# The last stage of a two-part image kernel: three column groups in a turn, a smaller output tile, and TensorE in program order

## The chip, the core and the metric

The kernel runs on one core of a Trainium2 chip, as one program. The metric is the device time of one execution in microseconds; the time shown is the median of several runs. A profile is a record of one execution: for each instruction on each engine its start and its length. The engines named here are TensorE (PE; its weight loads are PEld), VectorE (DVE), ScalarE (ACT), GpSimd (POOL) and SyncE (SP). They run side by side, each works through its own instructions in order, and they wait for each other by semaphores. TensorE writes its results into PSUM, which has eight banks of 128 x 512 floats; another engine has to read a bank out before it can be written again.

## What is computed

The input x has the shape (4, 64, 256, 256). Two layers follow each other. The first is an attention and feed-forward block with convolutions, and fills the first three quarters of the time. The second works on 64 channels (E) of every pixel and does linear attention along the rows, then the same along the columns, then a two-layer network. The last stage of the kernel does the column attention and the network. Cut to that, for the values of one column, with x of 256 rows and 64 channels:

```python
q = elu(n @ wq.T + bq) + 1          # 4 heads, one value each; n = layernorm(x)
k = elu(n @ wk.T + bk) + 1
v = n @ wv.T + bv                   # 4 heads of 16
q = q / q.mean(rows); k = k / k.sum(rows)
o = q * (k * v).sum(rows)
x = x + o @ wo.T + bo
x = x + gelu(layernorm(x) @ w1.T + b1) @ w2.T + b2
```

The output is x as (4, 64, 256, 256), with channels ahead of rows and columns.

## The kernel before

The kernel runs in five stages, and only the last, `stage_d`, is changed. It reads the result of the row attention from the scratch tensor `hd` in DRAM and writes `out`.

**Tiling.** There are 4 images and 8 groups of 32 columns in each, so 32 groups, in the list `seq`. A group is one tile `h` of 128 partitions by 32 columns by 2 row halves by 64 channels: the partition is the row in a half. A loop over `r` from 0 to 7 goes through a group four columns at a time.

**Two generators.** `attn` (L1178) does the attention of a group, and `ffn` (L1276) the network of the group before. `_steps` takes them forward in turn, from one `yield` to the next. A pass of the outer loop (L1316) is called a turn: it loads the next group, runs `attn` for group n and `ffn` for group n - 1, and after every second group it stores.

`attn` has these parts:
- For each r it transposes four blocks of `h` (L1188), copies the result out on ScalarE to `xT` (L1190) and multiplies by the query and key weights (L1197, "scores"). After four r the scores are turned on VectorE (L1201). Beside this runs `spread`, which takes the sum over channels (L1163), subtracts the mean (L1165), squares on ScalarE (L1167) and sums again (L1168), to give the variance. `rstd` takes the root on ScalarE (L1173) and the reciprocal (L1175).
- The scores are scaled and shifted (L1204, L1205), `feature` applies min and Exp, L1214 makes `f`, and L1217 makes `kz`, the weighted keys.
- L1223 sums keys times `h` over the rows. L1227 and L1230 give the sums of f and the turned queries. VectorE makes `z` and `zn` (L1234 to L1241), TensorE turns it (L1244), `mix` applies the value and output weights (L687), and VectorE makes `bdm` (L1250).
- L1256 and L1259 make the attention's output, in four PSUM banks for each row half, and L1262 adds it into `h`.
- `spread` and `rstd` again, and L1273 gives `xf`, the normalised tile that the network reads.

`ffn` turns four blocks of `xf` (L1283), copies to `xfT` (L1285), does the first layer in four PSUM banks (L1296) with Gelu on ScalarE (L1298), puts the residual `h` (L1304) and the second layer (L1307) into one bank, and VectorE adds the bias b2 and writes the bank to the output tile `st` (L1309). The write is turned: four columns next to each other in `st`, for 128 rows, so that consecutive writes lie 256 bytes apart. `st` holds two groups, that is 64 columns, and GpSimd's queue sends it out in eight DMAs of 512 KB (L1332) with runs of 256 bytes in DRAM.

**What sets the order.** The program's text gives the instructions and what they depend on. The order in which each engine gets them is set by the framework's scheduler when the kernel is built, by priorities and estimated durations. Tiles of one name share a fixed number of buffers (`bufs`), and an instruction that writes a tile waits until its buffer is free. PSUM is shared out by two helpers: `mm()` gives one of six banks and `sm()` one of two.

Of the kernel before, what the change touches and what calls it, by code (L numbers as in the profile page):

```python
# [9 lines left out]
F32 = mybir.dt.float32  # L10
AF = mybir.ActivationFunctionType
ALU = mybir.AluOpType
# [235 lines left out]
def kernel(ctx: ExitStack, tc: tile.TileContext, x, packs, fd, out, off):  # L248
# [8 lines left out]
    def mm():  # L257
        return ps.tile([128, 512], F32, tag="mm", name="mm")

    def sm():  # L260
        return ps.tile([128, 512], F32, tag="sm", name="sm", bufs=2)
# [33 lines left out]
    def bc(ap, n):  # L295

        return ap.unsqueeze(2).to_broadcast([ap.shape[0], ap.shape[1], n])
# [826 lines left out]
    def stage_d():  # L1124
        with ExitStack() as cs:
# [25 lines left out]
            V.memset(one, 1.0)  # L1151

            def load(b, g):
                h = p.tile([128, 32, 2, C], F32, name="h", bufs=3)
                for rh in (0, 1):
                    for j in (0, 1):
                        SY.dma_start(h[:, 16 * j:16 * j + 16, rh, :], hd[b, rh * 128:(rh + 1) * 128, :, 2 * g + j, :])
                return h

            def spread(src, n, s2):  # L1160

                s1 = p.tile([128, n], F32, tag="ln_s", name="ln_s")
                V.tensor_reduce(s1, src, AX.X, ALU.add)  # L1163
                xc = p.tile([128, n, C], F32, tag="xc", name="xc")
                V.scalar_tensor_tensor(xc, bc(s1, C), -LN_S, src, ALU.mult, ALU.add)  # L1165
                sq = p.tile([128, n, C], F32, tag="ln_sq", name="ln_sq")
                S.activation(sq, xc, AF.Square)  # L1167
                V.tensor_reduce(s2, sq, AX.X, ALU.add)  # L1168
                return xc

            def rstd(s2, n):
                s3 = p.tile([128, n], F32, tag="ln_d", name="ln_d")
                S.activation(s3, s2, AF.Sqrt, bias=eps_t, scale=LN_S)  # L1173
                s4 = p.tile([128, n], F32, tag="ln_r", name="ln_r")
                V.reciprocal(s4, s3)  # L1175
                return s4

            def attn(h, xfs):  # L1178

                qp = p1.tile([128, 32, 32], F32, name="qp")  # L1180
                v1 = p1.tile([128, 64], F32, name="v1")
                for r in range(8):
                    if r % 2 == 0:
                        k = r // 2
                        spread(h[:, 8 * k:8 * k + 8].rearrange("p c a e -> p (c a) e"), 16, v1[:, 16 * k:16 * k + 16])
                    t = mm()
                    for i in range(4):
                        T.transpose(t[:, i * 128:(i + 1) * 128], h[:, r * 4 + i].rearrange("p a e -> p (a e)"), ident)  # L1188
                    xT = p.tile([128, 512], F32, name="xT")
                    S.copy(xT, t)  # L1190
                    yield
                    if r % 4 == 0:
                        qk = sm()


                    for g in range(4):
                        T.matmul(qk[g * 32:(g + 1) * 32, r % 4 * 128:r % 4 * 128 + 128], cwt, xT.rearrange("p (c n) -> p c n", c=4)[:, :, g * 32:(g + 1) * 32],  # L1197
                                 start=True, stop=True)
                    if r % 4 == 3:

                        V.transpose(qp[:, r // 4 * 16:r // 4 * 16 + 16].rearrange("p c m -> p (c m)"), qk)  # L1201
                rs = rstd(v1, 64)
                u = qp[:, :, 0:16].rearrange("p c (r k) -> p c r k", r=2)
                V.tensor_tensor(u, u, bc4(rs, 2, 8), ALU.mult)  # L1204
                V.tensor_tensor(u, u, cbq.unsqueeze(1).unsqueeze(1).to_broadcast([128, 32, 2, 8]), ALU.add)  # L1205
                yield
                e = feature(p1, u, [128, 32, 2, 8])
                yield
                f = p1.tile([128, 2, 2, 32, 4], F32, name="f")
# [2 lines left out]
                for rh in (0, 1):  # L1212
                    for k in (0, 1):
                        V.scalar_tensor_tensor(f[:, rh, k], uv[:, rh, :, k * 4:k * 4 + 4], 1.0, ev[:, rh, :, k * 4:k * 4 + 4], ALU.add, ALU.max)  # L1214
                fv = f.rearrange("p r k c h -> p r k (c h)")
                kz = p1.tile([128, 2, 128], F32, name="kz")
                V.tensor_tensor(kz.rearrange("p r (c h) -> p r c h", h=4), f[:, :, 1], rs.rearrange("p (c r) -> p r c", r=2).unsqueeze(3).to_broadcast([128, 2, 32, 4]), ALU.mult)  # L1217
                yield

                t = mm()  # L1220
                for rh in (0, 1):
                    for g in range(4):
                        T.matmul(t[g * 32:(g + 1) * 32, :], kz[:, rh, g * 32:(g + 1) * 32], h[:, 8 * g:8 * g + 8, rh, :], start=(rh == 0), stop=(rh == 1))  # L1223
                qs = sm()
                for k in (0, 1):
                    for rh in (0, 1):
# [36 lines left out]
                    yield  # L1263
                for hf in (0, 1):
                    v2 = p.tile([128, 32], F32, name="v2")
                    xcs = []
                    for k in (2 * hf, 2 * hf + 1):
                        xcs.append(spread(h[:, 8 * k:8 * k + 8].rearrange("p c a e -> p (c a) e"), 16, v2[:, (k % 2) * 16:(k % 2) * 16 + 16]))
                        yield
                    rs = rstd(v2, 32)  # L1270
                    for k in (0, 1):
                        xf = p.tile([128, 8, 2, C], F32, name="xf", bufs=5)
                        V.tensor_tensor(xf.rearrange("p c a e -> p (c a) e"), xcs[k], bc(rs[:, k * 16:k * 16 + 16], C), ALU.mult)  # L1273
                        xfs.append(xf)

            def ffn(h, xfs, st, gi):  # L1276


                def first(r):
                    t = mm()  # L1280
                    xf = xfs[r // 2]
                    for i in range(4):
                        T.transpose(t[:, i * 128:(i + 1) * 128], xf[:, (r % 2) * 4 + i].rearrange("p a e -> p (a e)"), ident)  # L1283
                    xT = p.tile([128, 512], F32, name="xfT")
                    S.copy(xT, t)  # L1285
                    return xT

                yield
                xT = first(0)
                for r in range(8):  # L1290
                    yield
                    hg = []
                    for i in (0, 1):
                        for rh in (0, 1):
                            t = mm()
                            T.matmul(t, w1[rh * 64:(rh + 1) * 64, i * 128:(i + 1) * 128], xT[rh * 64:(rh + 1) * 64], start=True, stop=True)  # L1296
                            g = p.tile([128, 512], F32, tag=f"hg{rh}{i}", name=f"hg{rh}{i}")
                            S.activation(g, t, AF.Gelu, bias=b1[:, i:i + 1])  # L1298
                            hg.append(g)
                    nx = first(r + 1) if r < 7 else None  # L1300
                    yield
                    y = mm()
                    for i in range(4):
                        T.matmul(y[:, i * 128:(i + 1) * 128], h[:, r * 4 + i].rearrange("p a e -> p (a e)"), ident, is_transpose=True, start=(i == 0), stop=False, skip_group_check=True)  # L1304
                    for i in (0, 1):
                        for rh in (0, 1):
                            T.matmul(y[rh * 64:(rh + 1) * 64, :], w2[:, i, :], hg[i * 2 + rh], start=False, stop=(i == 1), skip_group_check=True)  # L1307
                    c = gi * 32 + r * 4
                    V.tensor_scalar(st[:, :, c:c + 4].rearrange("p r c -> p c r"), y.rearrange("p (c r) -> p c r", c=4), K("b2"), None, ALU.add)  # L1309
                    xT = nx  # L1310

            seq = [(b, g) for b in range(B) for g in range(8)]
            hs = {0: load(*seq[0])}
            xfs = {}
            st = None
            for n in range(len(seq) + 1):  # L1316
                if n + 1 < len(seq):
                    hs[n + 1] = load(*seq[n + 1])
                xfs[n] = []
                ga = attn(hs[n], xfs[n]) if n < len(seq) else None  # L1320
                gf = None
                if n >= 1:
                    b, g = seq[n - 1]
                    if g % 2 == 0:
                        st = p.tile([128, 128, 64], F32, name="st")
                    gf = ffn(hs.pop(n - 1), xfs.pop(n - 1), st, g % 2)
                _steps(ga, gf)
                if n >= 1 and g % 2 == 1:
                    for i in range(4):
                        for rh in (0, 1):  # L1330
                            r = rh * 128 + i * 32
                            G.dma_start(out[b, :, r:r + 32, g // 2 * 64:g // 2 * 64 + 64], st[rh * 64:(rh + 1) * 64, i * 32:(i + 1) * 32])  # L1332

    stage_d()

# [19 lines left out]
```

## Time and profile before

| | |
|---|---|
| median of 3 runs | 9063.34 us (9060.01 to 9071.98) |
| profiled execution, its own time | 9063.4 us |
| its span, first to last instruction | 9061.6 us |
| mean granted clock of TensorE | 0.974 |
| last stage, first work on `h` | 6817.9 us |
| last stage, last write to `st` | 9033.2 us, 1.07 us long |
| one turn of the last stage | 68.29 us |
| DMAs from `hd`: number, size, median time to landing | 128, 512 KB, 5.5 us |
| DMAs to `out`: number, size, median time to landing | 128, 512 KB, 12.0 us |

The table says where the stage begins and ends, and that it is a repetition: the turn is the distance between the starts of L1223 of one group and of the next. Rows of a group of instructions name the line, the engine, the operation, the tiles written and read, the shape, the count, then busy time in us and the mean of one in ns, and last the idle time of the engine just before them with the instruction that ended it. In a timeline a row has the start, the length, the same names, and in brackets the idle time before it.

### The profile page before, as it was taken

How to read it: one execution, taken by the hardware profiler on the slowest of the kernel's cores; microseconds unless marked ns; L12 is line 12 of the kernel's file. 1: busy time of each engine (PE TensorE's matmuls, PEld its weight loads, DVE VectorE, ACT ScalarE, POOL GpSimd, SP SyncE). 2: the span in 40 equal slices, each digit the busy share in tenths (PEclk: the TensorE clock that was granted, in tenths of full speed). 3: DMA queues.
4: the chain of work that ended last, by engine and by line, in shares of the span. 5: the costliest groups of instructions: out<-in, count | busy, mean ns of one | idle time of the engine just before them, and what ended most of it. 6: DMA issues, size and time to landing. Idle time of an engine off the chain costs nothing. (4 is left out here: it accounts for less than half of the span.)

```text
span 9061.6 us, 136047 instructions
## 1 busy us (share of the span) xinstructions
PE 8382.1 (93%) x53934; PEld 4354.5 (48%) x53934; DVE 5945.5 (66%) x8509; ACT 4740.4 (52%) x7844; POOL 1135.0 (13%) x1828
## 2 busy tenths in 40 slices
PE   8999999789999998999999999999997888898897
PEld 7877777534444443333333344444453333333333
DVE  6666666467777775222222288888887778878876
ACT  4455555545555554222222266666655767766765
POOL 1111111112221221000000011111110000000000
PEclk9999999889999999999999999999998999999999
DMA  6677767599999998888888855555533233233232
GB/s 149 138 178 173 173 168 172 152 317 384 391 393 392 382 388 333 297 297 296 297 297 297 279 163 172 173 172 168 168 117 69 53 66 66 55 66 64 58 66 47
DMA packets 1258475, 1831.95 MB, mean 202 GB/s; under 512 B 335600, under 2 KB 1040112, under 8 KB 1196656
## 3 DMA queue, kind: packets, MB, share of 16 engines
q1 hardware_dynamic: 1053296, 1034.55, 37.8%
q0 software_dynamic: 204544, 788.69, 26.6%
q8 instruction: 428, 7.01, 0.3%
q14 instruction: 207, 1.70, 0.1%
HBM read 967.57 MB, written 788.53 MB: 194 GB/s over the span
## 5 line engine op out<-in xcount | busy, mean ns | idle before, releaser
L900 DVE TENSOR_TENSOR y<-ge,mm 128x512 f32<-128x512 f32 (+1 forms) x640 | 406.2, 635 | 1212.2 <-ACT ge L899 1212.2
L867 PE MATMUL mm<-t,w 128*128 128x512 f32 (+1 forms) x2560 | 1093.9, 566 | 19.6 <-DMA t<-td 19.6
L899 ACT ACTIVATE ge<-mm 128x512 f32<-128x512 f32 (+1 forms) x640 | 354.7, 554 | 1253.8 <-PE mm L874 1253.8
L1298 ACT ACTIVATE hg<-mm,b 128x512 f32<-128x512 f32 x1024 | 631.7, 685 | 332.6 <-PE mm L1296 330.7
L760 PE MATMUL mm<-gp,wc 128*64 128x510 f32 (+1 forms) x3072 | 702.0, 595 | 89.4 <-DVE xm L770 51.2
L867 PEld LDWEIGHTS mm<-t,w 128*128 128x128 f32 x2560 | 455.4, 190 | 648.1 <-issue 437.5
L604 PEld LDWEIGHTS mm<-wqk,gp 128*128 128x128 f32 x6144 | 711.6, 192 | 71.2 <-issue 42.4
L604 PE MATMUL mm<-wqk,gp 128*128 128x128 f32 x6144 | 733.3, 276 | 0.0
L1307 PE MATMUL mm<-hg,pack_d 128*64 128x512 f32 x2048 | 579.4, 609 | 100.7 <-ACT hg L1298 100.7
L1296 PE MATMUL mm<-xfT,w 64*128 64x512 f32 x2048 | 638.4, 666 | 4.8 <-ACT xfT L1285 4.2
L815 ACT COPY tb<-mm 128x512 f32<-128x512 f32 x512 | 300.2, 587 | 632.3 <-PE mm L809 632.0
L874 PE MATMUL mm<-t,w 64*64 64x504 f32 (+1 forms) x5120 | 575.6, 555 | 0.0
L809 PE MATMUL mm<-xl,pack_c 64*128 64x512 f32 x2048 | 511.8, 599 | 8.9 <-ACT xl L797 4.7
L760 PEld LDWEIGHTS mm<-gp,wc 128*64 128x64 f32 x3072 | 278.1, 137 | 468.0 <-issue 330.2
L314 ACT ACTIVATE ln_sq<-xn 128x1024 f32<-128x1024 f32 x256 | 274.4, 1072 | 347.1 <-DVE xn L312 347.0
L316 DVE TENSOR_REDUCE ln_v<-ln_sq 128x16 f32<-128x1024 f32 x256 | 311.9, 1219 | 147.2 <-ACT ln_sq L314 147.2
L955 PE MATMUL mm<-ya,pack_e 128*64 128x512 f32 x1024 | 381.1, 616 | 11.2 <-DMA ya<-yd 11.2
L1309 DVE TENSOR_SCALAR st<-mm,pack_d 128x512 f32<-128x512 f32 x256 | 279.1, 1090 | 169.8 <-PE mm L1307 169.8
L1167 ACT ACTIVATE ln_sq<-xc 128x1024 f32<-128x1024 f32 x256 | 266.9, 1055 | 219.9 <-DVE xc L1165 219.7
L813 DVE COPY tb<-mm 128x512 f32<-128x512 f32 x512 | 344.9, 685 | 22.3 <-PE mm L809 16.8
L1296 PEld LDWEIGHTS mm<-xfT,w 64*128 64x128 f32 x2048 | 220.9, 202 | 272.4 <-issue 159.5
L874 PEld LDWEIGHTS mm<-t,w 64*64 64x64 f32 x5120 | 158.1, 132 | 374.4 <-issue 374.4
(455 smaller groups left out, 15547.3 us busy)
## 6 DMA issues: line engine op xcount, KB each, us to landing
t<-td SPq DMA_DIRECT2D x256, 1152.0 KB, 10.5
td<-tb POOLq DMA_DIRECT2D x144, 1024.0 KB, 16.1
td<-tb POOLq DMA_DIRECT2D x288, 512.0 KB, 13.9
yd<-y POOLq DMA_DIRECT2D x128, 1152.0 KB, 10.1
ya<-yd SPq DMA_DIRECT2D x192, 512.0 KB, 5.7
xs<-in_x_dram SPq DMA_DIRECT2D x128, 512.0 KB, 6.7
projd<-pj POOLq DMA_DIRECT2D x256, 256.0 KB, 4.8
gp<-projd SPq DMA_DIRECT2D x128, 512.0 KB, 9.5
```

Source lines behind the costliest of these rows:

```text
L604: T.matmul(qp[:, k * 128:(k + 1) * 128], gp[:, 2 * i + k // 2, at + dx:at + dx + 128], wqk[:, dx, :], start=(dx == 0), stop=(dx == 2))
L760: T.matmul(tv[i * 64:(i + 1) * 64, :, o], wc[2 * pr + i][:, dx, :], gps[i][:, 2 * r:2 * r + 2, i_], start=(dx == 1), stop=False, skip_grou ...
L809: T.matmul(t, inT[q, hf * 128:(hf + 1) * 128], xls[b // 2, s][q, :, 2 * y:2 * y + 2].rearrange("p f y t -> p f (y t)"), start=True, stop=True)
L813: V.tensor_copy(o, i_)
L867: T.matmul(t[:, :n], w[:, 0:128], x_[:, c, :], start=True, stop=False, skip_group_check=True)
L874: T.matmul(t[po:po + 64, :n].rearrange("p (n c) -> p n c", c=64)[:, :, o], w[q:q + 64, 128:192], x_[q:q + 64, c, i_], start=False, stop=Tr ...
L899: S.activation(ge[:, :n], ts[0][k][:, :n], AF.Gelu)
L900: V.tensor_tensor(y[:, c, :].rearrange("p n c -> p (n c)"), ge[:, :n], ts[1][k][:, :n], ALU.mult)
L955: T.matmul(t[b * 64:(b + 1) * 64, :], owT, ya[:, :, 2 * r:2 * r + 2, b * 64:(b + 1) * 64].rearrange("p f y t -> p y f t"), start=True, sto ...
L1296: T.matmul(t, w1[rh * 64:(rh + 1) * 64, i * 128:(i + 1) * 128], xT[rh * 64:(rh + 1) * 64], start=True, stop=True)
L1298: S.activation(g, t, AF.Gelu, bias=b1[:, i:i + 1])
L1307: T.matmul(y[rh * 64:(rh + 1) * 64, :], w2[:, i, :], hg[i * 2 + rh], start=False, stop=(i == 1), skip_group_check=True)
```

## The change

The stage is written anew around the same operations. `attn` becomes two generators, `scores` (up to `kz`) and `result` (from L1223 to `xf`), and `ffn` becomes three functions: `turn` (transposes of `xf` and their copy), `first` (first layer and Gelu) and `second` (residual, second layer, bias, store). A turn now holds `scores` of group n + 1, `result` of group n and the network of group n - 1. `i` counts r over all groups; in each iteration `first` is called for i + 1, `second` for i and `turn` for i + 2, and the generators are taken one step forward twice.

The whole loop stands in `tc.manual_schedule` for TensorE: its instructions are issued in the order of the program's text. The other engines are still ordered by the scheduler.

Further edits: `spread` takes two parts at a time and puts both second sums (the old L1168) behind both squares; `h` has four buffers and is loaded two turns ahead; `xf` has six; `st` holds one group of 32 columns, is written by ScalarE (`Identity` with a bias) and no longer by VectorE, with consecutive writes 128 bytes apart, and is stored after each group in four DMAs of 64 rows, with runs of 128 bytes in DRAM.

```diff
-                h = p.tile([128, 32, 2, C], F32, name="h", bufs=3)
+                h = p.tile([128, 32, 2, C], F32, name="h", bufs=4)
...
+            def spread(h, ks, v):
+                xcs, sqs = [], []
+                for k in ks:
+                    src = h[:, 8 * k:8 * k + 8].rearrange("p c a e -> p (c a) e")
...
+                    V.tensor_reduce(s1, src, AX.X, ALU.add)
...
+                    V.scalar_tensor_tensor(xc, bc(s1, C), -LN_S, src, ALU.mult, ALU.add)
...
+                    S.activation(sq, xc, AF.Square)
...
+                for i, k in enumerate(ks):
+                    V.tensor_reduce(v[:, 16 * i:16 * i + 16], sqs[i], AX.X, ALU.add)
+                return xcs
...
-            def attn(h, xfs):
+            def scores(n):
+                h = hs[n]
...
+                def up(r):
+                    t = mm()
+                    for i in range(4):
+                        T.transpose(t[:, i * 128:(i + 1) * 128], h[:, r * 4 + i].rearrange("p a e -> p (a e)"), ident)
+                    xT = p.tile([128, 512], F32, name="xT")
+                    S.copy(xT, t)
+                    return xT
...
+                xT = up(0)
+                spread(h, (0, 1), v1[:, 0:32])
+                yield
+                yield
+                qk = sm()
+                for r in range(7):
+                    if r == 4:
+                        back(0, qk)
+                        qk = sm()
+                    score(r, xT, qk)
+                    xT = up(r + 1)
+                    yield
+                    if r < 5:
+                        if r == 4:
+                            spread(h, (2, 3), v1[:, 32:64])
+                        yield
+
+                score(7, xT, qk)
+                back(1, qk)
                 rs = rstd(v1, 64)
...
+                fks[n] = f, kz
+
+            def result(n):
+                h = hs[n]
+                f, kz = fks.pop(n)
                 yield
...
                 for hf in (0, 1):
                     v2 = p.tile([128, 32], F32, name="v2")
-                    xcs = []
-                    for k in (2 * hf, 2 * hf + 1):
-                        xcs.append(spread(h[:, 8 * k:8 * k + 8].rearrange("p c a e -> p (c a) e"), 16, v2[:, (k % 2) * 16:(k % 2) * 16 + 16]))
-                        yield
+                    xcs = spread(h, (2 * hf, 2 * hf + 1), v2)
+                    yield
                     rs = rstd(v2, 32)
                     for k in (0, 1):
-                        xf = p.tile([128, 8, 2, C], F32, name="xf", bufs=5)
+                        xf = p.tile([128, 8, 2, C], F32, name="xf", bufs=6)
...
+            def turn(i):
+                n, r = divmod(i, 8)
+                t = mm()
...
+                S.copy(xT, t)
+                xTs[i] = xT
+
+            def first(i):
...
+            def second(i):
...
-                    V.tensor_scalar(st[:, :, c:c + 4].rearrange("p r c -> p c r"), y.rearrange("p (c r) -> p c r", c=4), K("b2"), None, ALU.add)
+                S.activation(st[:, :, 4 * r:4 * r + 4].rearrange("p r c -> p c r"), y.rearrange("p (c r) -> p c r", c=4), AF.Identity, bias=K("b2"))
+                if r == 7:
+                    b, g = seq[n]
+                    for q in (0, 1):
                         for rh in (0, 1):
...
+                            y0 = rh * 128 + q * 64
+                            G.dma_start(out[b, :, y0:y0 + 64, g * 32:g * 32 + 32], sts[n][rh * 64:(rh + 1) * 64, q * 64:(q + 1) * 64])
+                    del hs[n]
...
+            with tc.manual_schedule(engines={mybir.EngineType.PE}):
+                for n in range(-1, N + 1):
+                    if 0 <= n + 2 < N:
+                        hs[n + 2] = load(*seq[n + 2])
+                    gs = scores(n + 1) if n + 1 < N else iter(())
+                    gr = result(n) if 0 <= n < N else iter(())
+                    for r in range(8):
+                        i = 8 * (n - 1) + r
+                        if 0 <= i + 1 < 8 * N:
+                            first(i + 1)
+                        next(gs, 0)
+                        next(gr, 0)
+                        if 0 <= i < 8 * N:
+                            second(i)
+                        if 0 <= i + 2 < 8 * N:
+                            turn(i + 2)
+                        next(gs, 0)
+                        next(gr, 0)
+                    _steps(gs, gr)
```

More of the change, by code (lines that the diff above doesn't have):

```diff
@@ L1158, in load, with rstd @@
                 return h
[L1160 to L1171, printed above, removed]
+            def spread(h, ks, v):
+                xcs, sqs = [], []
+                for k in ks:
+                    src = h[:, 8 * k:8 * k + 8].rearrange("p c a e -> p (c a) e")
+                    s1 = p.tile([128, 16], F32, tag="ln_s", name="ln_s")
+                    V.tensor_reduce(s1, src, AX.X, ALU.add)
+                    xc = p.tile([128, 16, C], F32, tag="xc", name="xc")
+                    V.scalar_tensor_tensor(xc, bc(s1, C), -LN_S, src, ALU.mult, ALU.add)
+                    sq = p.tile([128, 16, C], F32, tag="ln_sq", name="ln_sq")
+                    S.activation(sq, xc, AF.Square)
+                    xcs.append(xc)
+                    sqs.append(sq)
+                for i, k in enumerate(ks):
+                    V.tensor_reduce(v[:, 16 * i:16 * i + 16], sqs[i], AX.X, ALU.add)
+                return xcs
+            def rstd(v, n):
                 s3 = p.tile([128, n], F32, tag="ln_d", name="ln_d")
-                S.activation(s3, s2, AF.Sqrt, bias=eps_t, scale=LN_S)
+                S.activation(s3, v, AF.Sqrt, bias=eps_t, scale=LN_S)
                 s4 = p.tile([128, n], F32, tag="ln_r", name="ln_r")
@@ L1176, in rstd @@
                 return s4
-            def attn(h, xfs):
+            def scores(n):
+                h = hs[n]
                 qp = p1.tile([128, 32, 32], F32, name="qp")
                 v1 = p1.tile([128, 64], F32, name="v1")
[L1182 to L1185, printed above, removed]
+                def up(r):
                     t = mm()
@@ L1190, in attn, with score @@
                     S.copy(xT, t)
-                    yield
-                    if r % 4 == 0:
-                        qk = sm()
+                    return xT
+                def score(r, xT, qk):
                     for g in range(4):
@@ L1198, in attn, with back @@
                                  start=True, stop=True)
-                    if r % 4 == 3:
-                        V.transpose(qp[:, r // 4 * 16:r // 4 * 16 + 16].rearrange("p c m -> p (c m)"), qk)
+                def back(k, qk):
+                    V.transpose(qp[:, k * 16:k * 16 + 16].rearrange("p c m -> p (c m)"), qk)
+                xT = up(0)
[16 more added lines that the diff above has]
+                back(1, qk)
                 rs = rstd(v1, 64)
@@ L1205, in attn @@
                 V.tensor_tensor(u, u, cbq.unsqueeze(1).unsqueeze(1).to_broadcast([128, 32, 2, 8]), ALU.add)
-                yield
                 e = feature(p1, u, [128, 32, 2, 8])
@@ L1214, in attn @@
                         V.scalar_tensor_tensor(f[:, rh, k], uv[:, rh, :, k * 4:k * 4 + 4], 1.0, ev[:, rh, :, k * 4:k * 4 + 4], ALU.add, ALU.max)
-                fv = f.rearrange("p r k c h -> p r k (c h)")
                 kz = p1.tile([128, 2, 128], F32, name="kz")
                 V.tensor_tensor(kz.rearrange("p r (c h) -> p r c h", h=4), f[:, :, 1], rs.rearrange("p (c r) -> p r c", r=2).unsqueeze(3).to_broadcast([128, 2, 32, 4]), ALU.mult)
+                fks[n] = f, kz
+            def result(n):
+                h = hs[n]
+                f, kz = fks.pop(n)
                 yield
@@ L1223, in attn @@
                         T.matmul(t[g * 32:(g + 1) * 32, :], kz[:, rh, g * 32:(g + 1) * 32], h[:, 8 * g:8 * g + 8, rh, :], start=(rh == 0), stop=(rh == 1))
+                fv = f.rearrange("p r k c h -> p r k (c h)")
                 qs = sm()
@@ L1265, in attn @@
                     v2 = p.tile([128, 32], F32, name="v2")
-                    xcs = []
-                    for k in (2 * hf, 2 * hf + 1):
-                        xcs.append(spread(h[:, 8 * k:8 * k + 8].rearrange("p c a e -> p (c a) e"), 16, v2[:, (k % 2) * 16:(k % 2) * 16 + 16]))
-                        yield
+                    xcs = spread(h, (2 * hf, 2 * hf + 1), v2)
+                    yield
                     rs = rstd(v2, 32)
                     for k in (0, 1):
-                        xf = p.tile([128, 8, 2, C], F32, name="xf", bufs=5)
+                        xf = p.tile([128, 8, 2, C], F32, name="xf", bufs=6)
@@ L1273, in attn @@
                         V.tensor_tensor(xf.rearrange("p c a e -> p (c a) e"), xcs[k], bc(rs[:, k * 16:k * 16 + 16], C), ALU.mult)
[L1274 to L1290, printed above, removed]
-                    yield
-                    hg = []
-                    for i in (0, 1):
-                        for rh in (0, 1):
[L1295 to L1310, printed above, removed]
@@ L1312, in stage_d @@
-            seq = [(b, g) for b in range(B) for g in range(8)]
[L1313 to L1332, printed above, removed]
+                        xfs[n, 2 * hf + k] = xf
@@ new lines, in result @@
+                    yield
+            def turn(i):
+                n, r = divmod(i, 8)
+                t = mm()
+                xf = xfs[n, r // 2]
+                for k in range(4):
+                    T.transpose(t[:, k * 128:(k + 1) * 128], xf[:, (r % 2) * 4 + k].rearrange("p a e -> p (a e)"), ident)
+                xT = p.tile([128, 512], F32, name="xfT")
+                S.copy(xT, t)
+                xTs[i] = xT
+            def first(i):
+                xT = xTs.pop(i)
+                hgs[i] = []
+                for k in (0, 1):
+                    for rh in (0, 1):
+                        t = mm()
+                        T.matmul(t, w1[rh * 64:(rh + 1) * 64, k * 128:(k + 1) * 128], xT[rh * 64:(rh + 1) * 64], start=True, stop=True)
+                        g = p.tile([128, 512], F32, tag=f"hg{rh}{k}", name=f"hg{rh}{k}")
+                        S.activation(g, t, AF.Gelu, bias=b1[:, k:k + 1])
+                        hgs[i].append(g)
@@ new lines, in second @@
+            def second(i):
+                n, r = divmod(i, 8)
+                h, hg = hs[n], hgs.pop(i)
+                if r == 0:
+                    sts[n] = p.tile([128, 128, 32], F32, name="st")
+                st = sts[n]
+                y = mm()
+                for k in range(4):
+                    T.matmul(y[:, k * 128:(k + 1) * 128], h[:, r * 4 + k].rearrange("p a e -> p (a e)"), ident, is_transpose=True, start=(k == 0), stop=False, skip_group_check=True)
+                for k in (0, 1):
+                    for rh in (0, 1):
+                        T.matmul(y[rh * 64:(rh + 1) * 64, :], w2[:, k, :], hg[k * 2 + rh], start=False, stop=(k == 1), skip_group_check=True)
+                S.activation(st[:, :, 4 * r:4 * r + 4].rearrange("p r c -> p c r"), y.rearrange("p (c r) -> p c r", c=4), AF.Identity, bias=K("b2"))
+                if r == 7:
+                    b, g = seq[n]
+                    for q in (0, 1):
+                        for rh in (0, 1):
+                            y0 = rh * 128 + q * 64
+                            G.dma_start(out[b, :, y0:y0 + 64, g * 32:g * 32 + 32], sts[n][rh * 64:(rh + 1) * 64, q * 64:(q + 1) * 64])
+                    del hs[n]
@@ new lines, in stage_d @@
+            seq = [(b, g) for b in range(B) for g in range(8)]
+            N = len(seq)
+            hs, fks, xfs, xTs, hgs, sts = {}, {}, {}, {}, {}, {}
+            hs[0] = load(*seq[0])
+            with tc.manual_schedule(engines={mybir.EngineType.PE}):
[17 more added lines that the diff above has]
+                    _steps(gs, gr)
```

## The prediction

> **What bounds it now.** I read the page first: the last stage is the part of the span from about 6818 us on. The list of waits and the chain of waits show it repeating every 68.29 us (the matmuls of L1223 start at 7041.44, 7109.73, 7178.02), once for each of 32 column groups, so I took one turn apart. Busy times of the turn (length, then PE, PEld, DVE, ACT, POOL, granted clock, DMA share, GB/s):
>
> ```profile
> 7041.44:7109.73 68.29, 60.75 (x350) 26.63 (x350) 54.54 (x67) 47.31 (x70) 0.10 (x1) 0.98 0.14 32
> ```
>
> No engine is full; TensorE is nearest. Its timeline in that turn shows what "busy" hides. Start, length, line, count, then the idle time before:
>
> ```profile
> 7047.11 1.99 PE L1296 MATMUL mm<-xfT,w 64*128 64x512 f32 x8
> ...
> 7065.97 2.81 PE L1307 MATMUL mm<-hg,pack_d 128*64 128x512 f32 x8 [1.62 <-ACT hg L1298]
> ...
> 7074.40 0.66 PE L1283 MATMUL mm<-pack_k,xf 128*128 128x128 f32 x4 [3.32 <-DVE xf L1273]
> ...
> 7075.79 3.48 PE L1296 MATMUL mm<-xfT,w 64*128 64x512 f32 x8 [0.29 <-ACT xfT L1285]
> ```
>
> The same eight matmuls take 1.99 us once and 3.48 another time. ScalarE's timeline says why: it loads a table and squares while PSUM banks wait for a gelu.
>
> ```profile
> 7076.24 1.28 ACT L1298 ACT_TABLE_LOAD   x1
> 7077.89 0.69 ACT L1298 ACTIVATE hg<-mm,b 128x512 f32<-128x512 f32 x1 [0.37 <-PE mm L1296]
> 7078.48 1.99 ACT L1167 ACTIVATE ln_sq<-xc 128x1024 f32<-128x1024 f32 x2
> 7080.37 1.83 ACT L1298 ACTIVATE hg<-mm,b 128x512 f32<-128x512 f32 x3
> ```
>
> TensorE's undisturbed pitches (start to next start in that timeline): F, the eight of L1296, 1.92; Y, L1304 with L1307, 0.53 + 1.87 = 2.40; X, four transposes of L1283, 0.49; up, four of L1188, 0.49; score, eight of L1197, 0.36; L1223 1.86; L1227 0.91; L1230 0.25; L1244 0.25; L687 0.44; L1256 with L1259, 0.96 + 0.97 = 1.93, twice. Sum: 8 x 5.66 + 3.71 + 3.86 = 52.9 us. So 15.4 us of a turn are waits, open or hidden in stretched matmuls.
>
> **The change, part by part.**
>
> *Three groups, F one and X two iterations ahead.* In program order an iteration r issues F(i+1), a step of scores and result, Y(i), X(i+2), another step. The xf tiles are made in the second half of iterations 3 and 4 and first read at 6, so the 3.3 us wait on xf goes; Y reads gelus of the iteration before, so the 3.2 us wait on hg goes. The stretched matmuls wait for banks, and stay as far as ScalarE is late.
>
> *Bias eviction from VectorE to ScalarE*, 8 a turn. VectorE falls to 54.5 - 8 x 1.09 = 45.8 us and is no bound. ScalarE's price isn't in the trace; nearest rows (line, engine, operation, tiles, count, busy us, mean ns):
>
> ```profile
> L1309 DVE TENSOR_SCALAR st<-mm,pack_d 128x512 f32<-128x512 f32 x256 | 279.1, 1090 | 169.8 <-PE mm L1307 169.8
> ...
> L797 ACT ACTIVATE xl<-mm,pack_c 128x256 f32<-128x256 f32 x512 | 333.5, 811 | 0.8 <-PE mm L795 0.8
> L549 ACT ACTIVATE pj<-mm,bin__121 128x512 f32<-128x512 f32 x256 | 174.2, 682 | 83.3 <-PE mm L547 77.0
> L899 ACT ACTIVATE ge<-mm 128x256 f32<-128x256 f32 x128 | 49.1, 384 | 134.4 <-PE mm L874 134.4
> ```
>
> L549 (with bias, contiguous) is the low end, 0.68 us. L797 writes single floats far apart, as st is written: 811 - (384 + 98 for a bias, from gelu's 685 against the copy's 587) = 329 ns over 256 elements, 1.29 ns each, so 682 + 512 x 1.29 = 1.34 us, the high end. The Trainium skill ("ScalarE: Activation LUTs", What ACT_TABLE_LOAD costs) says 280 ns + 0.833 ns an element with a bias pointer, 0.71 us, whatever the function, with no word of the destination; "SBUF — State Buffer" (Door 1) says each access to a new 16-byte line pays. L797 sides with the second, so I take 1.35: the same engine, the same write. ScalarE then has 47.3 + 8 x 1.35 = 58.1 us a turn, more than TensorE's 52.9; by the first page's rule it has 53.0, and the sum below would end at 8827 us instead of 8904. The row speaks against the change, and it becomes the bound.
>
> *ScalarE's load is uneven.* One iteration's evictions: four gelus 2.42, xT 0.59, xfT 0.59, st 1.35 = 4.95 us. Iterations 3 to 7 have five of these (24.8), three of the four square pairs (3 x 1.99 = 6.0), two roots with a table load each way (2 x 2.88 = 5.8), and root and Exp at the end with four loads (5.1 + 0.35 + 0.63 = 6.1): 42.7 us, against TensorE's 5 x 5.66 + 0.36 = 28.7. Iterations 0 to 2 are TensorE's: 8.32 (F, up, Y, X, L1223 to L1230), 6.35 (with L1244, L687) and 9.52 (two of 1.93) = 24.2, plus 1.3 where F of iteration 3 needs two more of the four banks whose adds (L1262) take 2.48; ScalarE needs only some 18 there. End to end 68.2. TensorE runs ahead by its six banks, about one iteration's evictions, 4.9 us, so the two stretches overlap by that: **63.3 us a turn**. With 0.68 us an eviction it is 68.2 - 3.4 - 4.2 = 60.6; with no overlap 68.2.
>
> *spread in pairs, xf and h with one buffer more*: same instructions, priced at nothing; L1168 waited 1.7 us for squares in the whole stage. If squares come late, v is late, hidden by one and a half iterations before xf is read.
>
> *Loads two turns ahead*: SyncE has only these in its queue, each lands in 5.5 us (median), a turn ahead of need.
>
> *Output tile of one group.* 128 stores of 512 KB as before, but runs of 128 bytes, not 256.
>
> ```profile
> q0 software_dynamic: 19008, 68.17, 15.1%
> ```
>
> That is 0.151 x 2262 us x 16 engines for 266,000 runs: 20.5 ns a run. The skill's "DMA: Bandwidth & Descriptors" (Specifications) wants at least 512 bytes for line rate and so speaks against the change too. At an unchanged price per run the stores take 524,288 x 20.5 ns / 16 = 672 us of some 2100, beside loads at 13%: hidden, and st's second buffer has a turn to empty. Only the last store shows. Now it is:
>
> ```profile
> 9034.65 8.74 POOL L1332 DMA_DIRECT2D out_dram<-st  x8 [108.47 <-DVE st L1309]
> ```
>
> with the end at 9061.6: 27 us, 16,384 runs. Then 4 issues, again 16,384 runs (21 us): no change; half-price runs would save 10 us, double cost 20. On GpSimd's queue behind the stores stands the memset of zn; it needs only the last L1244 and may go long before.
>
> *Filling and draining.* The first L1223 stays at 6840. The second came 65 us later; now there is no ffn between, only some 46 us of VectorE with its chain: 50, so -15. After the last L1223 it was 79 us to the last st (9034.2). Now the rest of a turn without scores (about 45), then eight iterations of ffn alone at 4.9 (now 4.81 apart): 84 to 85, +6. Together -9.
>
> **Sum.** 30 full turns x (63.3 - 68.29) = -150; -9; from the profiled execution, 9063.4 us with 1.8 outside its span: **8904 us**. The median of the runs shown is 9063.34, so nothing is to be shifted.
>
> **Rivals.**
> *A. The queues even out:* other work fills ScalarE's slack in iterations 0 to 2 and it alone bounds, 58.1 us: 30 x -10.2 - 9 = -315, 8749. For it: squares and roots have slack of an iteration or more. Against: six banks hold back TensorE.
> *B. TensorE's fixed order stalls at L1223, slower.* kz follows the last score through transpose, multiply, add, min, Exp, f. Before, from the second L1201 (7100.94) to kz's end (7109.58) it took 8.6 us, and 0.3 of it was seen. Now TensorE has Y, X, F, up, Y, X between, 8.2 us; then all behind L1223 stands, the next F and Y too, and ScalarE runs dry. If root and Exp each queue behind one iteration's evictions (4.95), the chain is 18.5 and TensorE stands 10.3 a turn: 73.6, 9213 us; with one of them 5.4: 68.7, 9067. Between: 9140. It decides from 5.9 us of standing a turn (69.2). Against: the root needs only v1, done an iteration earlier.
> *C. The overlap isn't there:* 68.2 us, about 9052, no change.
>
> **Chances.** The sum above 0.45 (8824 to 9052 by its ends), A 0.18, C 0.12, B 0.25. No change is within 0.2%, 18 us, about what this measurement can tell; C gives 0.05 to it, the rest of C is a small gain. Faster 0.70, same 0.05, slower 0.25. Range 8750 to 9120: it leaves half of A and a little under half of B outside.
>
> **What would show it.** Turns of L1223 about 63 us apart; st on ScalarE at about 1350 ns; no wait of L1283 for xf; ScalarE 56 to 58 us busy a turn, its idle time in iterations 0 to 2; stores at about 30% of the DMA engines; about 27 us from the last st to the end. Wrong if PE waits for kz by more than 2 us a turn (B), if st costs near 700 ns, or if turns are under 60 us.

## The result, and the profile after

| | before | after |
|---|---|---|
| median | 9064.61 us (4 runs) | 9342.46 us (9341.05 to 9351.75, 4 runs) |
| ratio to before, 95% interval | | 1.0308 (1.029 to 1.0326) |
| span of the profiled execution | 9061.6 us | 9341.2 us |
| mean granted clock of TensorE | 0.974 | 0.955 |
| one turn of the last stage | 68.29 us | 77.00 us |
| end of the last write to `st` to the end of the span | 27.3 us | 18.3 us |

The change makes the kernel slower by 3.1%; 8904 us was forecast, and 9342 lies outside the range. (The median before is that of the runs made beside it.) In the changed kernel L1313 is X, L1315 the copy `xfT`, L1324 F, L1326 the gelu, L1338 and L1341 Y, L1342 the write to `st`, L1254 the keys times `h`, L1195 and L1204 up and score.

The spans differ by 279.6 us. Thirty turns from the second L1254 to the last are worth 30 x (77.00 - 68.29) = 261; the second one starts 5 us later than before (6910.3 against 6904.9); and from the last one to the end it is 121 us, not 107, though the last store is 9 us quicker. The loss is in the turn. The thirty turns before and after (start and end, length, then busy PE, PEld, DVE, ACT, POOL, clock, DMA share, GB/s):

```profile
6904.86:8954.26 2049.40, 1828.01 (x10471) 803.61 (x10472) 1636.21 (x2010) 1421.04 (x2071) 134.15 (x150) 0.98 0.29 61
6910.31:9220.39 2310.08, 1872.06 (x10467) 817.36 (x10467) 1398.21 (x1764) 1664.33 (x2307) 198.09 (x150) 0.90 0.25 53
```

TensorE stands for 438 us in them, where before it stood for 221, and for the same matmuls it is busy for 44 us more.

TensorE's waits in the last stage, in the changed kernel (who waited on whom, us in total, times, longest):

```profile
PE mm L1324 <- ACT xfT L1315: 425.2, 193, 5.1
PE sm L1204 <- ACT xT L1197: 22.3, 36, 1.9
PE mm L1324 <- DVE h L1294: 21.9, 31, 0.7
PE mm L1254 <- DVE kz L1243: 17.9, 2, 10.6
PE mm L1313 <- DVE xf L1303: 5.2, 1, 5.2
```

One wait stands out: F waits for the copy `xfT`, 425 us in 193 waits. The waits forecast to go are gone: Y waits for no gelu, and X once for `xf`. The place where a rival looked for a stall, L1254 waiting for `kz`, has 17.9 us in two waits, as the stage fills.

One iteration of a turn shows how it comes about. TensorE's timeline, then ScalarE's over the same stretch (start, length, what, idle before and its releaser):

```profile
7632.79 0.66 PE L1313 MATMUL mm<-pack_k,xf 128*128 128x128 f32 x4
7636.75 3.62 PE L1324 MATMUL mm<-xfT,w 64*128 64x512 f32 x8 [3.30 <-ACT xfT L1315]
```

```profile
7634.18 1.06 ACT L1170 ACTIVATE ln_sq<-xc 128x1024 f32<-128x1024 f32 x1 [0.70 <-DVE xc L1168]
7635.15 1.12 ACT L1342 ACTIVATE st<-mm,pack_d 128x512 f32<-128x512 f32 x1
7636.07 0.62 ACT L1315 COPY xfT<-mm 128x512 f32<-128x512 f32 x1
7638.85 0.69 ACT L1326 ACTIVATE hg<-mm,b 128x512 f32<-128x512 f32 x1 [2.16 <-PE mm L1324]
```

X starts at 7632.79 and is done at 7633.45. ScalarE first waits for `xc` and squares, and then takes the write to `st`, which is ahead of the copy in its order; Y is ahead of X on TensorE. Only at 7636.07 does it copy, and 7636.07 + 0.62 is 7636.69. F starts at 7636.75: it reads the very copy of the X that stands directly ahead of it. TensorE has nothing between the two, so it stands for 3.30 us, and then ScalarE stands for 2.16 us for F. The two engines take turns instead of working side by side.

Here are the busy times of two parts of this turn, in the columns of the thirty turns above. The first part goes from the F behind L1262 to the X of iteration 3 and has three F; the second goes from there to the next L1254 and has five. The 3.1 us of L1254 to L1262 are in neither.

```profile
7608.85:7632.79 23.94, 22.59 (x141) 9.96 (x140) 12.71 (x21) 12.54 (x20) 0.10 (x1) 1.00 0.16 34
7632.79:7683.31 50.52, 37.01 (x187) 16.37 (x185) 33.19 (x38) 41.77 (x57) 6.52 (x4) 0.83 0.29 62
```

In the first part, where `result` puts matmuls between X and F, TensorE is busy for 22.6 of 23.9 us. In the second it is busy for 37.0 of 50.5 us, and ScalarE for 41.8: neither is full.

A part of the 37.0 is a second cost. Four pieces of the second part in the same columns: the wait, F behind it, what follows, and a later stretch behind a wait of 1.14 us.

```profile
7633.40:7636.70 3.30, 0.04 (x1) 0.00 (x0) 3.30 (x4) 2.59 (x4) 0.00 (x0) 1.00 0.00 0
7636.75:7640.40 3.65, 3.65 (x12) 1.28 (x16) 0.78 (x1) 1.53 (x2) 0.00 (x0) 0.54 0.02 4
7640.40:7644.20 3.80, 3.80 (x28) 1.82 (x28) 2.96 (x4) 3.76 (x6) 0.00 (x0) 1.00 0.00 0
7657.75:7662.00 4.25, 4.25 (x30) 2.08 (x32) 4.25 (x4) 4.23 (x7) 0.00 (x0) 1.00 0.00 0
```

F took 3.62 us behind the wait of 3.30 and 1.99 behind that of 1.14: the granted clock fell to 0.54 for one such stretch. The Trainium skill ("TensorE: Matmul & The Clock Gate", What's actually happening) has the clock at half after an idle window of about 3.4 us, and at full again after about 3.4 us of work. The rows agree in kind, though the wait here was 3.30 us. It is no sharp limit: at 7124.54 an F behind a wait of 1.42 us ran at 0.53. In the 3.41 us up to there TensorE had been busy for 1.48.

```profile
7124.54 3.68 PE L1324 MATMUL mm<-xfT,w 64*128 64x512 f32 x8 [1.42 <-ACT xfT L1315]
```

So waits of this length can be paid nearly twice.

The group rows (busy us, mean ns, then idle before):

```profile
L1324 PE MATMUL mm<-xfT,w 64*128 64x512 f32 x2048 | 704.5, 786 | 447.1 <-ACT xfT L1315 425.2
...
L1342 ACT ACTIVATE st<-mm,pack_d 128x512 f32<-128x512 f32 x256 | 292.5, 1142 | 229.9 <-PE mm L1341 229.6
```

F's mean is 786 ns where before it was 666, and ScalarE's write to `st` takes 1142 ns.

### The profile page after: what moved, and what is told of

It reads as the page before. It is cut to its first block, busy times and chain, and to the rows that moved or that the text cites. A ratio compares the mean times of both kernels' runs of the same rounds, so it can differ in the third digit from the quotient of the medians.

```text
span 9341.2 us, 136316 instructions
## 1 busy us (share of the span) xinstructions
PE 8437.7 (90%) x53934; PEld 4369.7 (47%) x53934; DVE 5695.8 (61%) x8253; ACT 5003.4 (54%) x8100; POOL 1203.9 (13%) x1828
## 5 line engine op out<-in xcount | busy, mean ns | idle before, releaser
L1324 PE MATMUL mm<-xfT,w 64*128 64x512 f32 x2048 | 704.5, 786 | 447.1 <-ACT xfT L1315 425.2
L1326 ACT ACTIVATE hg<-mm,b 128x512 f32<-128x512 f32 x1024 | 634.0, 688 | 276.6 <-PE mm L1324 275.0
L1324 PEld LDWEIGHTS mm<-xfT,w 64*128 64x128 f32 x2048 | 221.9, 225 | 719.9 <-ACT xfT L1315 485.5
L1341 PE MATMUL mm<-hg,pack_d 128*64 128x512 f32 x2048 | 498.0, 607 | 0.0
L1348 POOL DMA_DIRECT2D out_dram<-st x128 | 208.8, 1635 | 2066.0 <-ACT st L1342 1929.4
L1342 ACT ACTIVATE st<-mm,pack_d 128x512 f32<-128x512 f32 x256 | 292.5, 1142 | 229.9 <-PE mm L1341 229.6
L1174 DVE TENSOR_REDUCE v<-ln_sq 128x16 f32<-128x1024 f32 x256 | 304.0, 1208 | 49.8 <-ACT ln_sq L1170 49.5
```

Source lines behind the costliest of these rows:

```text
L1324: T.matmul(t, w1[rh * 64:(rh + 1) * 64, k * 128:(k + 1) * 128], xT[rh * 64:(rh + 1) * 64], start=True, stop=True)
L1326: S.activation(g, t, AF.Gelu, bias=b1[:, k:k + 1])
L1341: T.matmul(y[rh * 64:(rh + 1) * 64, :], w2[:, k, :], hg[k * 2 + rh], start=False, stop=(k == 1), skip_group_check=True)
L1342: S.activation(st[:, :, 4 * r:4 * r + 4].rearrange("p r c -> p c r"), y.rearrange("p (c r) -> p c r", c=4), AF.Identity, bias=K("b2"))
```

## The experiments

All are kernels of their own, timed against the kernel before in three rounds, ratios with their 95% intervals. Diffs are against the changed kernel unless another is named. "Turn" is the mean distance of L1254 over thirty turns of the profiled execution (in the one made from the kernel before, of L1223 over one).

### 1. X ahead of Y

```diff
-                        if 0 <= i < 8 * N:
-                            second(i)
                         if 0 <= i + 2 < 8 * N:
                             turn(i + 2)
+                        if 0 <= i < 8 * N:
+                            second(i)
```

> Only the order of two calls is turned: turn(i+2) ahead of second(i). Theory A (TensorE waits because, in its fixed order, the transposes X of one block stand directly ahead of the first layer F that reads them, with ScalarE's copy xfT between): the 425 us of F's wait for xfT go, and with them most of the half-clock stretches behind the waits; turn about 63 to 66 us instead of 77, total 8880 to 9000 us. Rival B (ScalarE's uneven load is what TensorE waits for, and xfT is only the last of a backlog): the wait moves to another tile (a gelu, a bank), turn above 73 us, total above 9230 us.

9038.36 us, ratio 0.9974 (0.9964 to 0.9984), turn 67.32 us: 304 us came back with two calls exchanged. In the iterations with the network alone, at the end of the stage, no other group's work interferes: `st` is written every 4.81 us here, every 6.09 in the changed kernel. The longest of the waits that are left:

```profile
PE mm L1324 <- ACT xfT L1315: 196.1, 124, 4.9
PE mm L1338 <- ACT hg L1326: 39.0, 29, 1.3
PE sm L1204 <- ACT xT L1197: 38.8, 30, 1.5
```

F's wait is less than half. The total is above theory A's range by 38 us and far below B's; the turn, too, is above A's by 1.3 us. The thirty turns of this kernel:

```profile
6903.44:8923.18 2019.74, 1729.23 (x10466) 777.35 (x10467) 1396.50 (x1764) 1657.80 (x2305) 194.23 (x148) 0.96 0.31 60
```

Of the 290 us by which they are shorter than in the changed kernel, 147 are standing time of TensorE, and 143 are matmuls that take longer there; the granted clock is 0.96 here and 0.90 there. Most of the 143 is the clock: an estimate from the trace's clock records, half of TensorE's busy time at half clock, gives 215 us there and 88 here. So the second cost is nearly as large as the first. The two parts of a turn in this kernel, up to Y of iteration 3 and from there to L1254:

```profile
7647.87:7669.02 21.15, 20.44 (x132) 9.60 (x132) 11.42 (x21) 10.81 (x19) 1.73 (x2) 1.00 0.36 63
7669.02:7712.54 43.52, 34.56 (x194) 14.78 (x193) 33.79 (x38) 43.07 (x59) 4.89 (x3) 0.92 0.29 61
```

Now ScalarE is busy for 43.1 of 43.5 us in the second part: the uneven load of rival B is real, once the wait that hid it is gone.

### 2. TensorE ordered by the scheduler

```diff
-            with tc.manual_schedule(engines={mybir.EngineType.PE}):
+            if True:
```

> The fixed order of TensorE is taken away, all else of the change stays; the scheduler orders TensorE. Theory A: the scheduler can put other work between X and F, so the wait shrinks; turn about 66 to 70 us, total 9000 to 9130 us. Rival B: ScalarE is no lighter, turn stays at 74 us or more, total above 9250 us.

9336.59 us, ratio 1.03 (1.0283 to 1.0317), turn 77.13 us: A's number was wrong, and B's was right for another reason. The scheduler left X behind Y, and where nothing had stood between X and F it put the scores alone, 0.43 us:

```profile
PE mm L1324 <- ACT xfT L1315: 299.7, 163, 6.3
PE sm L1259 <- DVE f L1241: 107.1, 32, 14.1
```

```profile
8007.04 0.66 PE L1313 MATMUL mm<-pack_k,xf 128*128 128x128 f32 x4
8007.78 0.43 PE L1204 MATMUL sm<-xT,cwt 128*32 128x128 f32 x8
8010.99 2.75 PE L1324 MATMUL mm<-xfT,w 64*128 64x512 f32 x8 [2.78 <-ACT xfT L1315]
```

Some waits moved to L1259 (sums of f), the time did not go. So taking the fixed order away gains nothing; in this program the scheduler keeps X where the text has it, behind Y.

### 3. The bias eviction back on VectorE

```diff
-                S.activation(st[:, :, 4 * r:4 * r + 4].rearrange("p r c -> p c r"), y.rearrange("p (c r) -> p c r", c=4), AF.Identity, bias=K("b2"))
+                V.tensor_scalar(st[:, :, 4 * r:4 * r + 4].rearrange("p r c -> p c r"), y.rearrange("p (c r) -> p c r", c=4), K("b2"), None, ALU.add)
```

> The bias eviction st goes back to VectorE, the order stays as in the changed kernel. Theory A: X and F still stand together, but the copy xfT no longer queues behind the 1.14 us of st: about 1 us less in each of the six iterations a turn that wait, turn about 70 to 71 us, total about 9130 to 9180 us, and F still waits for xfT. Rival B (ScalarE's load): 9.2 us less a turn on ScalarE, turn about 66 to 68 us, total 9000 to 9060 us.

9129.81 us, ratio 1.0073 (1.0058 to 1.0088), turn 69.98 us, at the lower edge of A's figures. F still waits, but 122 us less, and TensorE's busy time in thirty turns falls from 1872 to 1782 us; the two together are the 213 us by which this run is faster than the change:

```profile
PE mm L1324 <- ACT xfT L1315: 303.1, 164, 5.3
```

### 4. Both

The edits of 1 and 3 together.

> X ahead of Y, and st on VectorE. Theory A: little beyond the first of the two, since the wait is gone already: total within 60 us of that run, turn 61 to 65 us. Rival B: only this one of the four comes under 9000 us.

9055.18 us, ratio 0.9991 (0.9982 to 0.9999), turn 67.88 us. The total is within A's 60 us of run 1, the turn is longer than A's 61 to 65, and B's forecast failed. The eviction on ScalarE costs 213 us where X is behind Y (run 3 against the change) and nothing where X is ahead of it: this run, with VectorE, is 17 us slower than run 1. X behind Y costs 75 us with the eviction on VectorE (run 3 against this one), and 304 with it on ScalarE. So most of the loss is neither move alone but the two together: the eviction stands in the way of the copy that F waits for. With both undone, what is left of the change brings no gain that counts. From the end of iteration 3's F to the Y of the next turn's iteration 0:

```profile
7681.70:7723.30 41.60, 32.80 (x198) 14.71 (x198) 41.47 (x48) 35.69 (x49) 3.42 (x3) 0.96 0.22 50
```

VectorE is busy for 41.5 of 41.6 us: with `st` on it, VectorE is what is full in that stretch. TensorE's waits are for ScalarE's `xfT` (203 us) and `hg` (82), but ScalarE in turn waits 138 us for VectorE's `xc` in the thirty turns, 84 in run 1. That this is what takes the gain is argued from the waits; no run takes it apart.

### 5 and 6. X ahead of F, and a spread moved out of the full stretch

Run 5 puts `turn(i + 2)` at the head of the iteration, ahead of `first(i + 1)`. Run 6 adds to it:

```diff
-                        if r == 4:
+                        if r == 0:
                             spread(h, (2, 3), v1[:, 32:64])
```

> turn(i+2) is moved on, ahead of first(i+1), so that a whole iteration lies between X and the F that reads its copy. Theory A alone (what is left of F's wait for xfT, 196 us with X ahead of Y, is still the distance): the wait falls under 40 us, turn 64 to 65 us, total 8930 to 8970 us. Theory B2 (with X ahead of Y the stage is held by ScalarE, full from iteration 3 to 7): the wait moves to gelu or a bank, turn 66 to 68 us, total 9000 to 9040 us.

> As the run with X ahead of F, and spread(2, 3) of scores moved from iteration 5 to iteration 1: 7.2 us of VectorE and 2.0 us of ScalarE leave the full stretch and go where both stand idle. Theory B2 (uneven load): turn 2 to 4 us shorter than in that run, 60 to 120 us in total. Theory A: no more than 20 us.

Run 5: 9030.67 us, ratio 0.9962 (0.9947 to 0.9977), turn 66.88 us. F's wait for the copy is gone, and others stand in its place, as B2 had it:

```profile
PE sm L1204 <- ACT xT L1197: 115.4, 41, 3.6
PE mm L1195 <- ACT st L1342: 78.3, 59, 2.8
PE mm L1324 <- DVE h L1294: 22.6, 31, 0.7
PE mm L1324 <- ACT hg L1326: 21.7, 32, 2.0
```

Run 6: 8942.27 us, ratio 0.9864 (0.9849 to 0.9879), turn 64.16 us, 2.7 us shorter, inside B2's figures. The same work was done; 7.2 us of VectorE and 2.0 us of ScalarE in a turn were moved from iteration 5 to iteration 1, where both have idle time. Of the 82 us that thirty turns lose, 51 are TensorE's busy time (1779 to 1728 us, the granted clock from 0.96 to 1.00), the rest is standing.

### 7. `st` on VectorE in iterations 3 to 7 only

As run 6, with ScalarE's write for r < 3 and VectorE's for the others.

> As the run before in this list, and the bias eviction on ScalarE in iterations 0 to 2 and on VectorE in 3 to 7. Theory B2: ScalarE loses 5 x 1.14 us in its full stretch, VectorE gains 5 x 1.09 there and has room after the move of spread; turn 1 to 4 us shorter, 30 to 120 us in total. If VectorE is the one that is full there: the same or longer.

9045.55 us, ratio 0.998 (0.9972 to 0.9987): 103 us slower than run 6, a miss for B2; that VectorE may be what is full there was the other expectation. The new wait is rival B's own place:

```profile
PE mm L1254 <- DVE kz L1243: 107.2, 30, 12.5
```

VectorE makes `kz` at the end of the second part, with five evictions now in the same queue, and `kz` is late in nearly every turn. L1254 stands for 3.26 us and then takes 3.64 instead of 1.92:

```profile
7722.66 3.64 PE L1254 MATMUL mm<-h,kz 128*32 128x512 f32 x16 [3.26 <-DVE kz L1243]
```

Other waits shrink, so that TensorE stands in all about as long as in run 6; its busy time rises from 1728 to 1828 us in thirty turns, at a granted clock of 0.93 instead of 1.00.

### 8. The kernel before with the bias eviction on ScalarE

The edit of the change for L1309 alone, in the kernel before (there X stands between F and Y in the text, L1300).

> The kernel before, with only the bias eviction moved to ScalarE (two-group tile, writes 256 bytes apart). In the kernel before X stands between F and Y, so theory A says that the eviction does not delay the copy that F waits for: turn 66 to 70 us, total 9000 to 9110 us, and st near 1140 ns. Rival B (ScalarE's load as such): 9 us more on ScalarE lengthen the turn by 4 us or more, total above 9190 us.

9127.81 us, ratio 1.0072 (1.0055 to 1.0089), turn 70.52 us, `st` at 1142 ns: 65 us slower, between the two expectations, so it decides for neither. The move alone was a loss in the old schedule too, though F waits there for its copy for 0.7 us in the whole stage. TensorE's waits for `xT` (L1197) rise from 11.9 to 47.5 us; where the rest of the 65 us comes from was not followed up.

### 9 to 12. Fewer table loads, and the best order

Run 9 is run 6 with one root for all of `xf` (one `rstd(v2, 64)` and five `xc` buffers); run 10 also takes the root for the scores in iteration 3; run 11 is run 1 with the early spread of run 6; run 12 is run 11 with the one root of run 9.

> As the run with the early spread, and one root for both halves of the variance ahead of xf, so that two table loads and one root (2 x 1.28 + 0.32 us) less stand on ScalarE in a turn; the xc tile has five buffers for it. Theory B2 (ScalarE is what is full, 57 of 64.2 us): turn 2 to 3 us shorter, 60 to 90 us in total against the run with the early spread. If the waits left are chains and not ScalarE's load: within 20 us.

> As the run with one root, and the root for the scores taken in iteration 3 beside it, not at the turn's end, so that the two can share a table load. Theory B2: another 30 to 80 us less, turn about 60 to 61 us; the chain to kz also loses its root.

> X between F and Y as in the first run of the series, with the early spread. It tells whether the whole iteration between X and F is worth something once the load is more even. Theory A: F still waits for xfT in this order, 20 to 60 us slower than with X ahead of F. Theory B2: within 20 us of it, about 8930 to 8965 us.

> X between F and Y, early spread, and one root for both halves ahead of xf. With X ahead of F the one root brought nothing and a new wait of X for xf (79 us in the stage) stood in its place; with X half an iteration later that wait should be gone. If ScalarE's load is what is left: 2 to 3 us a turn less than with two roots, 8830 to 8870 us. If chains are left: 8900 to 8940 us.

| | us | ratio to before (interval) | turn, us |
|---|---|---|---|
| 9, one root | 8949.04 | 0.9875 (0.986 to 0.9889) | 64.32 |
| 10, roots together | 8960.83 | 0.9884 (0.9868 to 0.9901) | 64.62 |
| 11, X between F and Y, early spread | 8917.94 | 0.9841 (0.9826 to 0.9855) | 63.40 |
| 12, the same with one root | 8941.55 | 0.9863 (0.9846 to 0.9879) | 64.18 |

Fewer table loads brought nothing with X ahead of F and cost 24 us with X between F and Y; taking the roots together (run 10) brought nothing beyond it. In run 9 the root comes later for the first half of `xf`, and new waits take what was saved:

```profile
PE mm L1315 <- DVE xf L1304: 79.3, 29, 2.7
PE mm L1254 <- DVE kz L1243: 44.7, 30, 4.6
```

So beyond run 6 ScalarE's load alone isn't what is left; the new waits point to the chains to `xf` and `kz`. Run 11 is the best, and beats both kernels: 1.6% under the kernel before. Its two parts, the second here with L1254 to L1262 of the next turn:

```profile
7609.20:7630.00 20.80, 20.09 (x130) 9.25 (x130) 10.40 (x18) 10.76 (x17) 1.73 (x2) 1.00 0.38 68
7630.00:7672.70 42.70, 36.13 (x225) 16.35 (x222) 37.05 (x44) 41.68 (x58) 4.89 (x3) 0.96 0.30 67
```

The whole iteration between X and F was worth nothing once the load was evened: run 11 is 24 us faster than run 6, and 12 us under the lower of the two expectations for it.

## Why the prediction was wrong

**The step that failed** is "Three groups, F one and X two iterations ahead". It wrote down the order, F(i+1), Y(i), X(i+2), and struck off the waits for `xf` and for gelu, but put F's wait for the copy `xfT` at nothing, without a reason. X(i+2) is the last work of iteration i, and F(i+2) is the first of iteration i + 1: on TensorE they are neighbours wherever the generators have no matmuls in the second step. The kernel before had X between F and Y (L1300), so the edit moved X behind Y, and this move was not priced. With the eviction on ScalarE it costs 304 us by run 1, or 30 x (77.00 - 67.32) = 290 in the full turns. For the same reason "TensorE runs ahead by its six banks" failed: free banks don't help an engine whose next matmul needs a copy that hasn't been made. The two stretches did not overlap, and the turn is longer even than the 68.2 us worked out for no overlap: the second part took 50.5 us, where 42.7 of ScalarE's work had been counted.

**The first reading of the trace was part of it.** F at 3.48 us in the kernel before was put down to banks that wait for gelu. That stretch (7075.79 to 7079.20) had a granted clock of 0.55, and 3.32 us of waiting stood just ahead of it: it was the clock behind a wait. So a new wait of 3 us has its price and then half a stretch more, and the sum had no term for it.

**The uneven load was right**, and comes to light when the copy is out of the way: 42.7 us were worked out for ScalarE in iterations 3 to 7; it was busy for 41.8 in the second part of the changed kernel's turn, and run 1 took 43.5 us for that part with ScalarE full. Evening it brings 120 us (run 11 against run 1). Run 11's turn of 63.40 us is near the 63.3 of the sum, but by another way, with a spread moved, and doesn't confirm it.

**The eviction on ScalarE** was sized at 1.35 us and took 1.14, between the contiguous 0.68 and L797's price, and nearer to the latter than to the 0.71 that leaves the destination out. That ScalarE would become the bound by itself is wrong for the change: it was busy for 1664 of the 2310 us of thirty turns, 55.5 of 77.0 in a turn. What the eviction does is stand ahead of the copy, and this the prediction didn't ask: what is queued behind it on its engine.

**The waits for `xf` and gelu** went, as forecast. Their time was taken by other waits: run 4, where the wait for `xf` is gone but F waits 203 us for the copy and Y 82 us for gelu, is level with the kernel before.

**The output tile** was priced per run and pays per byte. In the full turns of the changed kernel the stores' queue has

```profile
q0 software_dynamic: 16526, 60.15, 13.8%
```

of 2213 us and 16 engines for 470,000 runs: 10.4 ns a run, half of the 20.5 before, 12.3 GB/s an engine where it was 12.5. The rule that short runs lose line rate is not contradicted, as no kernel here stores this tile in longer runs than 256 bytes, but from 256 to 128 bytes next to nothing more is lost. The last store ends 18.3 us after `st`, not 27; "half-price runs would save 10 us" was the end that came true.

```profile
9321.71 1.11 ACT L1342 ACTIVATE st<-mm,pack_d 128x512 f32<-128x512 f32 x1 [1.35 <-PE mm L1341]
9323.23 4.89 POOL L1348 DMA_DIRECT2D out_dram<-st  x3 [35.92 <-ACT st L1342]
9330.83 1.63 POOL L1348 DMA_DIRECT2D out_dram<-st  x1 [2.71 <-issue]
```

The stores before took 8.74 us of GpSimd for eight; one takes 1.63 us now, not 1.10. No run went back to the larger tile, so the tile's whole share wasn't measured by itself; nor was that of the squares in pairs or of the added buffers, which every run from 1 to 7 and 9 to 12 keeps.

**Filling and draining** were forecast at -9 us (-15 and +6) and are +19 (5.4 and 13.5, the quicker store included). Eight iterations of the network alone at 6.09 us instead of 4.81 are 10 of it, from the same cause as the turn. The first L1254, forecast to stay at 6840 us, comes at 6849.7, and the second 60.6 us later, not 50; why was not followed up.

**The rivals.** The side was rival B's, not its mechanism: TensorE stood for far more than the 5.9 us a turn from which B would have decided, but at F, not at L1254, where after the first two groups it waits for nothing. Run 7 shows that its place can decide, when VectorE is made late. In run 11 F still waits 141.6 us for the copy and L1254 about 1.2 us a turn for `kz`; what it would take to remove these is open: the scheduler's order on ScalarE and VectorE was left as it is.

## What to carry to other kernels

When a loop is written with work for i, i + 1 and i + 2, count the distance between a producer and its consumer in the order in which the engine gets them, across the loop's end: the last call of one iteration and the first of the next are neighbours, whatever their indices say. Before moving an eviction to an engine with idle time, ask which copy stands behind it there and who waits for it. And even out a turn by stretches: 7 us of VectorE and 2 us of ScalarE moved within a turn were worth more than the deeper pipeline.

## What was not expected of the hardware

A wait of 3.30 us on TensorE left the next stretch of 3.65 us at a granted clock of 0.54; one of 1.14 us left it at 1.00, but one of 1.42, with more standing close before it, left it at 0.53. In the change this cost nearly as much as the waits themselves (run 1). Runs of 128 bytes in DRAM moved at 12.3 GB/s an engine, runs of 256 at 12.5. And a write of single floats 128 or 256 bytes apart cost ScalarE 1142 ns for 128 x 512, the same at both distances (the change and run 8), against 682 for a contiguous one with a bias.
